# LSTM with residual: weight sums read in place, plain-block stores and plain products moved within the first steps

## Chip, core and metric

The kernel runs on one core of a Trainium2 chip. The metric is the device time of one execution in microseconds (us); lower is better. The profile names the engines PE (TensorE), DVE (VectorE), ACT (ScalarE), POOL (GpSimd) and SP (SyncE, which issues every DMA here); "PEld" is TensorE's weight load.

## What is computed

An LSTM over 512 time steps with batch 32 and width 512, whose output is added to its input:

```python
xW = jnp.einsum('ntd,dg->ntg', x, Wx) + b        # x: (32, 512, 512), Wx: (512, 2048)
def step(carry, xw_t):
    prev_h, prev_c = carry
    a = xw_t + prev_h @ Wh                        # Wh: (512, 2048)
    i, f, o = sigmoid of the first three quarters of a;  g = tanh of the last
    next_c = f * prev_c + i * g
    next_h = o * jnp.tanh(next_c)
    ...
out = x + lstm(x, cond_1024, Wx, Wh, b)
```

All data is float32. The steps depend on each other through `prev_h`; `xW` does not.

## The kernel before

**A step.** `h_part(t)` (L252) makes the hidden-state product: 32 matmul records on line 261 that add to a PSUM bank which already holds step t's row of xW plus bias. That row was copied there by `seed_step` (L692, ACT, line 699) from the small ring `xw`. `cell(t)` (L265) then runs the gates on ACT (L276 to L278, L283) and DVE (L280 to L287) and ends with the transposed state `ht` (L287), for which the next `h_part` waits. While the cell runs, TensorE works at the input product of later steps: that work is the "stream".

**The stream.** Steps 20 to 499 get their xW from 15 groups of 32 steps. A group is made by a fast bilinear scheme with 26 "slots". A slot multiplies one sum of x blocks (U, table `U_SUMS`, made on DVE at L476) by one sum of weight blocks (V, table `V_SUMS`) in seven products; DVE evacuates the results into `cbuf` and `r1` buffers with help of ACT (`evacuate`, L609: ACT L618, L627, L634; DVE L624, L628, L631) and combines them into output blocks (`w_op`, L402; DVE line 423), which go to DRAM (`xwd`, L439) and come back row by row (`load_xw`, L679). `items` (L531) lists all products in order: "row" n of this list holds the first two products of slot n, two of slot n-1, two of slot n-2 and the last of slot n-3, so that a full row has seven. `emit_matmuls(n)` (L541) issues the next n quarters of products (four quarters are one product, 8 records on line 562), and `pos` counts the quarters. `u_ahead(n)` (L603) makes the U sums that the next n quarters need. `seed_banks` (L586) copies bias seeds into the banks of some slots (`BIAS_OF`, ACT line 595).

**The weight sums.** V sums do not depend on the group: they are made once, in the first steps (`v_sum`, L758; DVE lines 734 and 737), in temporary rooms (`vroom`, L703; `V_ROOMS` says which room each sum takes), stored to DRAM (`v_store`, L740, L741), and read back for every group as ring rows (`load_v`, L649; three rows `vring`; lines 662 and 667). Eight slots (`V_DIRECT`) use a plain weight block instead of a sum; their parts come straight from Wx (L662) or are stored by `v_raw` (L765).

**The first 20 steps (the head).** Their xW is a plain product with bias: `plain_block` (L189, line 197). Steps 0 to 4 are done at the start; steps 5 to 19 come as listed in `HEAD_PLAINS`, two whole blocks in each of steps 0 to 4, one in steps 6 to 9. `HEAD_STREAM` (L45) gives the number of quarters streamed in each step from step 5 on; together 728, all of group 0. Each step is cut into chunks (L932 to L944): 24 quarters (16 in step 5), then a plain block, then at most 12 quarters at a time. `jobs` (L877 to L886) hangs the early DVE work and stores on steps: V sums in steps 0 to 4, the stores of six plain weight blocks in step 6, `late_seeds` (bias combinations, L792, DVE lines 786 to 798) in step 8.

**Order.** The program is scheduled by hand: every engine and SP's queue run their instructions in the order of emission. `room["dve"]` is a count of spare DVE time that decides how many `w_op` are emitted in a chunk.

**The end.** From step 468 the stream is over, and plain products for the last 12 steps (`plain_part`, L201) fill TensorE; their weights are loaded by `late_loads` (L222) at the steps `LATE` (L41).

Of the kernel before, what the change touches and what calls it, by code (L numbers as in the profile page):

```python
# [40 lines left out]
LATE = (453, 455, 457, 463, 465, 467, 469)  # L41
# [3 lines left out]
HEAD_STREAM = (0, 0, 0, 0, 0, 16, 40, 48, 56, 56, 60, 60, 60, 60, 60, 56, 52, 44, 32, 28)  # L45
# [14 lines left out]
V_ROOMS = (5, 0, 1, 2, 6, 3, 4, 0, 1, 2, 3, 7, 0, 6, 1, 4, 5, 2)  # L60
# [44 lines left out]
def kernel(  # L105
# [77 lines left out]
    def raw(blk):  # L183

        if late_weights[0]:
            return late_r[:, LATE_AT[blk]] if blk < 6 else r1[:, blk - 6]
        return r1[:, blk]
# [26 lines left out]

    def late_load(c, a, b):
        rows = wx[c].rearrange("p (j s c) -> p j s c", j=NJ, s=2)
        dst, n = (late_r, LATE_AT[a]) if a < 6 else (r1, a - 6)
        return lambda: nc.sync.dma_start(
            out=dst[:, n : n + b - a, c % 2 * 2 : c % 2 * 2 + 2], in_=rows[:, a % 4 : a % 4 + b - a]
        )  # L220
# [3 lines left out]
    late_loads += [late_load(2, 4, 6), late_load(3, 4, 6), late_load(2, 6, 8), late_load(3, 6, 8)]  # L224
# [86 lines left out]
    free_c = [NC, 0, 2, 4, 5, 8, 1, 3]  # L311
    last_x = []
    free_u = [0, 1, 2, 3, 6, 7, 4, 5]
# [87 lines left out]

    def w_op(short=False):  # L402
        first = wqueue[0]
# [29 lines left out]
        store_blocks()  # L433
# [107 lines left out]
    def emit_matmuls(n):  # L541

        while n > 0 and pos[0] < 4 * len(items):
# [17 lines left out]
            for j in range(4):  # L561
# [3 lines left out]
                    vring[:, row % 3, RIGHT[r], cols],  # L565
# [20 lines left out]
    def seed_banks(n):  # L586

        last = (pos[0] + n - 1) // 4
        while seeded[0] < len(items):
            row, slot, r = items[seeded[0]]  # L590
            if r == 1 and slot % R in BIAS_OF:
                late = seeded[0] > last
                if late and (pos[0] < 4 * bank_free(slot) or (slot - 5, 4) in finished or seeded[0] > last + 10):
                    return
# [54 lines left out]
    def load_v(row):  # L649
# [8 lines left out]
        for n, a, b in parts:  # L658
            while a < b:
                s, e = n - a // 2, b  # L660
                if row < 2 * R and a in (0, 2, 4) and s in V_DIRECT:
# [3 lines left out]
                if row < 2 * R:  # L665
                    e = next((k for k in (2, 4) if a < k < b and n - k // 2 in V_DIRECT), b)
                nc.sync.dma_start(out=vring[:, row % 3, a:e], in_=vdram[n, :, a:e])
                a = e

# [36 lines left out]
    vroom.append(xs0[:, 4:6].rearrange("p k s m -> p (k s m)")[:, 0 : 7 * HW].rearrange("p (k c) -> p k c", k=7))  # L706
# [51 lines left out]
    def v_sum(i):  # L758
        d = v_add(V_SUMS[i])
        vt[i] = d  # L760
        for s in range(R):
            if V_OF[s] == i:
                v_stores.append(lambda s=s: v_store(s, split_parts(vroom[d]), vroom[d]))

    def v_raw(s):  # L765
        v_store(s, v_parts(V_OF[s]))
# [8 lines left out]
    seed_rows = [cbuf[:, 6 + i // 2, i % 2 * 2 : i % 2 * 2 + 2].rearrange("p s c -> p (s c)") for i in range(4)]  # L775
    seed_rows += [seeds_own[:, i] for i in range(2)]
    names = ("-b2", "b0-b3", "b3", "b0-b1+b2", "b1", "b1-b0")
# [13 lines left out]

    def late_seeds():  # L792
        q = seed_rows
        split_seeds((1, 2, 3))
        sub(q[0], q[1], q[4])
        sub(q[1], q[1], q[2])
        add(q[3], q[0], q[3])
        sub(q[0], q[0], q[3])
# [27 lines left out]
    with tc.manual_schedule():  # L826
# [40 lines left out]
        for s in V_DIRECT[:2]:  # L867
            v_raw(s)
# [29 lines left out]
        for t in range(T):  # L898
# [18 lines left out]
            if t == 1:  # L917
# [6 lines left out]
            if t == 7:  # L924
                load_seeds(((1, 0), (3, 2), (2, 3)))
# [5 lines left out]
            if t < HEAD_STEPS:  # L931
# [3 lines left out]
                if t > 4:  # L935
                    chunks.append(("stream", {5: 16}.get(t, 24)))
                    left -= chunks[0][1]
                while plain or left:
                    if plain:
                        chunks.append(plain.pop(0))  # L940
                    m = 0 if plain and t <= 5 else min(left, 12)
                    if m:
                        chunks.append(("stream", m))
# [146 lines left out]
```

## Time and profile before

| what | value |
|---|---|
| median of 3 runs | 3096.03 us (3094.58 to 3096.34) |
| the profiled execution | 3094.41 us, span 3092.6 us |
| TensorE matmul busy | 3065.7 us, 99% of the span, 43600 records |
| DVE, ACT, POOL busy | 2350.3, 1473.6, 241.3 us |
| DMA | 756.94 MB, mean 245 GB/s |

How to read it: a row of the timeline gives start, duration (us), engine, line, operation, operands (out<-in), form and count, and in brackets the idle time before it with what ended it. Consecutive alike instructions are merged into one row. Ends of matmuls are modelled and overlap the next start by some tenths, so prices are best taken from start to start. A row of the table by stretches gives the stretch, its length, busy time and records of PE, PEld, DVE, ACT and POOL, the granted TensorE clock, the busy share of the DMA engines, and GB/s.

### The profile page before, as it was taken

What the parts mean: (1) busy time and instruction counts of PE and PEld (TensorE: products, weight loads), DVE (VectorE), ACT (ScalarE), POOL (GpSimd) and SP (SyncE); (2) the same over time, 40 slices, a digit from 0 to 9 for tenths busy, and PEclk for the clock granted to TensorE, in tenths of its full rate; (3) what the DMA queues carried; (4) which work ended last, traced back from release to release, by engine and by line L of the source; (5) the groups of instructions that cost most, each with busy time, mean ns of one, the idle gap of its engine ahead of it and who ended that gap; (6) DMA issues with size and microseconds to landing.
All of it is one profiled execution on the core that took longest, in us unless ns stands there. A gap on an engine that the chain in (4) does not pass through costs nothing.

```text
span 3092.6 us, 108381 instructions
## 1 busy us (share of the span) xinstructions
PE 3065.7 (99%) x43600; PEld 1654.6 (54%) x43600; DVE 2350.3 (76%) x6381; ACT 1473.6 (48%) x5528; POOL 241.3 (8%) x508
## 2 busy tenths in 40 slices
PE   9899999999999999999999999999999999999998
PEld 7654555555555555555555555555555555555665
DVE  8588787787877878778787787878778787787644
ACT  2344544445454444545445444454445545444444
POOL 0000000000000000000000000000000000000110
PEclk9999999999999999999999999999999999999999
DMA  9788878787777777778788787877878778788530
GB/s 360 253 288 265 280 249 272 236 264 239 250 257 249 256 243 248 260 238 270 235 258 262 226 268 241 260 249 242 266 240 265 238 249 260 246 265 259 170 91 22
DMA packets 320439, 756.94 MB, mean 245 GB/s; under 512 B 51008, under 2 KB 102720, under 8 KB 319424
## 3 DMA queue, kind: packets, MB, share of 16 engines
q1 hardware_dynamic: 319936, 750.00, 75.0%
q8 instruction: 344, 5.64, 0.8%
q14 instruction: 159, 1.30, 0.1%
HBM read 568.13 MB, written 184.81 MB: 243 GB/s over the span
## 4 chain that ended last, share of the span: by engine, by line
PE 94%; DVE 3%; DMA 2%; issue 1%; ACT 0%; SPq 0%; DVEq 0%; ACTq 0%
PE gbank L261 53%; PE xbank L562 32%; PE bbank L562 5%; PE xbank L261 2%; PE xbank L206 1%; DMA r<-in_L_cond_Wx_dram 1%; DMA vdram<-vring 1%; DVE vring L737 0%; DVE ubuf L737 0%; DVE prod L280 0%; PE gbank L197 0%; DMA vring<-vdram 0%; DVE s L281 0%; DMA vdram<-ubuf 0%; DVE ht L287 0%
## 5 line engine op out<-in xcount | busy, mean ns | idle before, releaser
L261 PE MATMUL gbank<-wh_sb,ht 128*32 128x512 f32 (+1 forms) x16288 | 1780.3, 575 | 5.3 <-DVE ht L287 3.4
L261 PEld LDWEIGHTS gbank<-wh_sb,ht 128*32 128x32 f32 x16288 | 606.3, 110 | 834.9 <-issue 703.6
L562 PE MATMUL xbank<-vring,ubuf 128*32 128x256 f32 (+1 forms) x13632 | 855.3, 369 | 8.8 <-issue 5.2
L276 ACT ACTIVATE s<-gbank 128x128 f32<-128x128 f32 x976 | 274.0, 281 | 1222.0 <-PE gbank L261 1221.4
L562 PEld LDWEIGHTS xbank<-vring,ubuf 128*32 128x32 f32 x13632 | 530.6, 110 | 300.4 <-issue 141.4
L280 DVE TENSOR_TENSOR prod<-s 128x128 f32<-128x128 f32 x1024 | 293.9, 287 | 489.1 <-ACT s L277 484.5
L295 POOL TENSOR_TENSOR oc<-xnat,ht 128x128 f32<-128x128 f32 x504 | 241.1, 478 | 2813.4 <-DVE ht L287 1349.8
L283 ACT ACTIVATE tanh_c<-s 128x64 f32<-128x64 f32 x1024 | 262.5, 257 | 244.0 <-DVE s L281 241.4
L287 DVE STREAM_TRANSPOSE ht<-hbuf 128x64 f32<-128x64 f32 x1022 | 250.9, 245 | 76.9 <-DVE hbuf L285 2.9
L699 ACT COPY gbank<-xw 128x512 f32<-128x512 f32 x459 | 275.9, 601 | 4.9 <-DMA xw<-xwd 4.8
L281 DVE TENSOR_TENSOR s<-prod 128x64 f32<-128x64 f32 x1024 | 230.3, 225 | 35.2
L285 DVE TENSOR_TENSOR hbuf<-o,tanh_c 128x64 f32<-128x64 f32 x1024 | 211.9, 207 | 31.3 <-ACT tanh_c L283 30.7
L277 ACT ACTIVATE s<-gbank 128x64 f32<-128x64 f32 x976 | 226.0, 232 | 0.0
L562 PE MATMUL xbank<-vring,xs 128*32 128x256 f32 (+1 forms) x3216 | 209.4, 357 | 3.4 <-DMA vring<-in_L_cond_Wx_dram 1.8
L562 PE MATMUL xbank<-vring,r 128*32 128x256 f32 (+1 forms) x3216 | 208.4, 357 | 0.0
L562 PE MATMUL bbank<-vring,ubuf 128*32 128x256 f32 (+1 forms) x2608 | 185.7, 342 | 0.0
L562 PEld LDWEIGHTS xbank<-vring,r 128*32 128x32 f32 x3216 | 123.5, 110 | 78.7 <-issue 46.2
L562 PEld LDWEIGHTS xbank<-vring,xs 128*32 128x32 f32 x3216 | 124.7, 110 | 64.0 <-issue 23.8
L423 DVE TENSOR_TENSOR cbuf<-cbuf 128x1024 f32<-128x1024 f32 x130 | 157.9, 1218 | 0.6
L278 ACT ACTIVATE o<-gbank 128x128 f32<-128x128 f32 (+1 forms) x509 | 155.5, 305 | 0.0
L562 PEld LDWEIGHTS bbank<-vring,ubuf 128*32 128x32 f32 x2608 | 102.2, 110 | 66.5 <-issue 38.3
L423 DVE TENSOR_TENSOR r<-r 128x1024 f32<-128x1024 f32 x104 | 127.5, 1226 | 0.8
(136 smaller groups left out, 2546.9 us busy)
## 6 DMA issues: line engine op xcount, KB each, us to landing
vring<-vdram SPq DMA_DIRECT2D x311, 896.0 KB, 5.7
xw<-xwd SPq DMA_DIRECT2D x1920, 64.0 KB, 4.4
xwd<-r SPq DMA_DIRECT2D x116, 512.0 KB, 4.7
xwd<-cbuf SPq DMA_DIRECT2D x114, 512.0 KB, 4.7
out_dram<-oc SPq DMA_DIRECT2D x255, 128.0 KB, 4.2
xnat<-in_x_dram SPq DMA_DIRECT2D x62, 512.0 KB, 6.6
xs<-in_x_grouped_dram SPq DMA_DIRECT2D x45, 512.0 KB, 4.5
vring<-vdram SPq DMA_DIRECT2D x35, 512.0 KB, 5.0
```

Source lines behind the costliest of these rows:

```text
L261: nc.tensor.matmul(dst[j * B : (j + 1) * B], state["ht"][:, k], m, start=False, stop=True, skip_group_check=True)
L276: nc.scalar.activation(s[:, u, 0:2], g[:, n_, 0:2], AF.Sigmoid)
L277: nc.scalar.activation(s[:, u, 2], g[:, n_, 3], AF.Tanh)
L280: nc.vector.tensor_mul(prod[:, u], s[:, u, 0:2], s[:, u, 2:4])
L281: add(nxt[:, u, 3], prod[:, u, 0], prod[:, u, 1])
L283: nc.scalar.activation(tanh_c[:, HALVES[u]], nxt[:, u, 3], AF.Tanh)
L285: nc.vector.tensor_mul(hbuf[:, HALVES[u]], o[:, u], tanh_c[:, HALVES[u]])
L287: nc.vector.transpose(ht[:, 2 * u : 2 * u + 2].rearrange("p q b -> p (q b)"), hbuf[:, HALVES[u]])
L295: (nc.gpsimd if t < T - 8 else nc.vector).tensor_add(oc[:, tt % 2], x_of(t), ht)
L423: op(c_of(dst), c_of(src), c_of(bb))
L562: nc.tensor.matmul(dst[j * B : (j + 1) * B, cols], left_of(gr, s, r)[:, j * B : (j + 1) * B], vring[:, row % 3, RIGHT[r], cols], start=sta ...
L699: nc.scalar.copy(bank_of(t), src)
```

## The change

1. The first four slots (`HELD = 4`) read their weights where they were made: sums 9 and 10 in their rooms (vring 0, ubuf 6 and 7), plain blocks 5 and 0 in r1 and cbuf. No ring rows are loaded for them in group 0, and buffers that hold them come free with their last product. `V_ROOMS` is new, with two more rooms in `xs0`; the x rows 0 and 1 load in step 2 instead of 1.
2. The stores of all plain blocks, and of sums 9 and 10, which later groups need, move to steps 5 to 7. Before, two plain blocks were stored ahead of step 0, six in step 6, and the two sums when they were made.
3. From step 5 on, a plain product comes in four pieces, each followed by a share of the stream; `HEAD_STREAM` has other numbers with the same sum.
4. Seeds: one in step 8, the rest in step 10, in other buffers. `seed_step` of the next step is emitted ahead of the first stream chunk's matmuls (for step 20, behind cell 19) instead of at the end of the step. In the head, finished output blocks are stored at the start of a chunk instead of at once.
5. The last late weights load into free buffers at step 468 instead of 469 into r1.

The diff, cut to its core:

```diff
-LATE = (453, 455, 457, 463, 465, 467, 469)
+LATE = (453, 455, 457, 463, 465, 467, 468)
-HEAD_STREAM = (0, 0, 0, 0, 0, 16, 40, 48, 56, 56, 60, 60, 60, 60, 60, 56, 52, 44, 32, 28)
+HEAD_STREAM = (0, 0, 0, 0, 0, 24, 52, 48, 56, 56, 56, 56, 56, 56, 56, 56, 48, 44, 36, 28)
+HELD = 4
-V_ROOMS = (5, 0, 1, 2, 6, 3, 4, 0, 1, 2, 3, 7, 0, 6, 1, 4, 5, 2)
+V_ROOMS = (5, 0, 6, 8, 1, 3, 9, 2, 4, 7, 3, 2, 7, 4, 1, 3, 2, 5)
...
+    def last_load(c):
+        rows = wx[c].rearrange("p (j s c) -> p j s c", j=NJ, s=2)
+        while len(late_more) < 2:
+            late_more.append(buf_of(take(free_c)))
+        for n in range(2):
+            nc.sync.dma_start(out=late_more[n][:, c % 2 * 2 : c % 2 * 2 + 2], in_=rows[:, 2 + n])
...
-    free_c = [NC, 0, 2, 4, 5, 8, 1, 3]
+    free_c = [NC, 2, 4, 1, 3, 6, 7]
-    free_u = [0, 1, 2, 3, 6, 7, 4, 5]
+    free_u = [0, 1, 2, 3, 4, 5]
...
     def w_op(short=False):
+        if short and done_blocks:
+            store_blocks()
+            return
...
-        store_blocks()
+        if not wait_to_store[0]:
+            store_blocks()
...
-                    vring[:, row % 3, RIGHT[r], cols],
+                    right_of(row, slot, RIGHT[r])[:, cols],
...
                 if r == 4:
                     left_done(gr, s)
+                    if slot < HELD:
+                        (free_u if slot == 1 else free_c).extend({1: (6, 7), 2: (V_OF[2],), 3: (V_OF[3],)}.get(slot, ()))
+
+    def right_of(row, slot, k):
+        if slot >= HELD:
+            return vring[:, row % 3, k]
+        return v_parts(V_OF[slot])[2] if k == 6 else v_parts(V_OF[slot])[k % 2][:, k // 2]
...
                 s, e = n - a // 2, b
+                if row < 2 * HELD and s < HELD:
+                    a = min(a + 2, b)
+                    continue
...
-            if V_OF[s] == i:
+            if V_OF[s] == i and s >= HELD:
                 v_stores.append(lambda s=s: v_store(s, split_parts(vroom[d]), vroom[d]))
...
-        for s in V_DIRECT[:2]:
-            v_raw(s)
...
-        jobs[3] = [lambda: load_v_to(1)] + [lambda: pair_sum(0, (0, 1))] * 4 + [lambda: u_ahead(8)] + sums(24)
+        jobs[3] = [lambda: pair_sum(0, (0, 1))] * 4 + [lambda: u_ahead(8)] + sums(24)
-        jobs[6] = [lambda s=s: v_raw(s) for s in V_DIRECT[2:]]
-        jobs[8] = [late_seeds]
-        jobs[9] = [lambda: load_row(0, 3), lambda: free_c.extend(range(NC + 1, NC + 7))]
+        raws = lambda *ids: [lambda s=s: v_raw(s) for s in ids]
+        jobs[5] = raws(0, 7, 17, 24)
+        jobs[6] = raws(1, 8, 15, 21)
+        jobs[7] = raws(2, 3)
+        jobs[8] = [second_seeds]
+        jobs[10] = [late_seeds]
...
-            if t == 1:
+            if t == 2:
                 load_row(0, 0)
                 load_row(0, 1)
...
+                pieces = [(k, p, cs) for k, p in plain for cs in (((0, 1, 2, 3),) if t < 5 else ((0,), (1,), (2,), (3,)))]
+                while pieces or left:
+                    m = min(left, 12)
+                    if pieces:
+                        chunks.append(pieces.pop(0))
+                        m = -(-left // (4 * len(pieces) + 4)) * 4
                     if m:
-                        chunks.append(("stream", m))
+                        chunks.append(("stream", m, None))
                         left -= m
...
                         load_v_ahead()
+                        store_blocks()
                         u_ahead(m)
...
                         seed_banks(m)
+                        if i == 0 and t + 1 in SEEDED and t + 1 < HEAD:
+                            seed_step(t + 1)
                         emit_matmuls(m)
                         room["dve"] += m * PROD / 4
                         if i == 0:
                             cell(t)
+                            if t + 1 == HEAD:
+                                seed_step(t + 1)
                             room["dve"] -= 2500.0
                             while todo and not plains:
                                 todo.pop(0)()
...
-                if t + 1 in SEEDED:
-                    seed_step(t + 1)
```

`second_seeds` splits one bias row and makes one seed (3 DVE operations); the new `late_seeds` splits two rows and makes the other three seeds (5 operations).

More of the change, by code (lines that the diff above doesn't have):

```diff
@@ L593, in seed_banks @@
                 if late and (pos[0] < 4 * bank_free(slot) or (slot - 5, 4) in finished or seeded[0] > last + 10):
+                    return
+                if BIAS_OF[slot % R] not in seeds_made:
+                    assert late
                     return
@@ L665, in load_v, with known @@
                 if row < 2 * R:
-                    e = next((k for k in (2, 4) if a < k < b and n - k // 2 in V_DIRECT), b)
+                    e = next((k for k in (2, 4, 6) if a < k < b and known(row, n - k // 2, k)), b)
                 nc.sync.dma_start(out=vring[:, row % 3, a:e], in_=vdram[n, :, a:e])
                 a = e
+    def known(row, s, k):
+        return row < 2 * HELD and s < HELD or k < 6 and s in V_DIRECT
     def load_v_to(row):
@@ L946 @@
                 todo = jobs.pop(t, [])
-                plains = sum(k == "plain" for k, _ in chunks)
-                for i, (kind, m) in enumerate(chunks):
+                plains = sum(k == "plain" for k, *_ in chunks)
+                for i, (kind, m, cs) in enumerate(chunks):
                     if kind == "plain":
-                        room["dve"] = 3000.0
-                        for cc in range(4):
+                        room["dve"] = max(room["dve"], 0.0) + PLAIN * len(cs) / 4
+                        for cc in cs:
                             plain_block(m, cc, plain_bank(m), True)
@@ L960 @@
                             flush_v()
+                        if not plains:
+                            for f in ends.get(t, ()):
+                                f()
                     else:
                         load_v_ahead()
+                        store_blocks()
                         u_ahead(m)
@@ L1000 @@
             n = target
+            wait_to_store[0] = False
             if t == HEAD_STEPS:
```

51 lines of the change are left out of this document (33 added, 18 removed).

## The prediction

> **What bounds the kernel now.** The page comes first, then a table by step (each stretch runs from the start of one step's hidden-state product to the next), then TensorE's timeline.
>
> ```profile
> PE 3065.7 (99%) x43600; PEld 1654.6 (54%) x43600; DVE 2350.3 (76%) x6381; ACT 1473.6 (48%) x5528; POOL 241.3 (8%) x508
> ```
> ```profile
> 29.55:81.25 51.70, 51.70 (x806) 38.41 (x801) 46.50 (x90) 14.82 (x50) 5.07 (x5) 1.00 1.03 370
> 81.25:87.82 6.57, 5.85 (x71) 2.41 (x62) 2.77 (x9) 2.74 (x10) 0.00 (x0) 1.00 0.97 353
> 87.82:102.70 14.88, 11.64 (x176) 6.79 (x180) 4.71 (x16) 4.27 (x14) 0.91 (x2) 1.00 0.85 289
> 102.70:116.76 14.06, 12.35 (x199) 8.89 (x193) 5.55 (x18) 4.62 (x14) 0.46 (x1) 1.00 1.05 350
> 116.76:132.99 16.23, 13.18 (x215) 9.32 (x209) 10.70 (x25) 4.30 (x14) 0.46 (x1) 1.00 0.51 167
> 155.83:166.82 10.99, 10.16 (x159) 6.74 (x152) 9.98 (x24) 5.71 (x17) 1.15 (x1) 1.00 1.03 390
> 206.34:216.82 10.48, 9.46 (x140) 4.31 (x136) 9.24 (x21) 4.23 (x15) 0.46 (x1) 1.00 0.77 262
> 225.03:234.62 9.59, 7.40 (x100) 3.26 (x96) 7.08 (x18) 3.16 (x12) 1.15 (x1) 0.96 0.79 272
> 234.62:243.40 8.78, 8.02 (x93) 3.71 (x85) 4.96 (x15) 3.74 (x13) 0.46 (x1) 0.85 0.82 253
> 260.00:2880.00 2620.00, 2619.32 (x36232) 1372.27 (x36228) 2056.81 (x5581) 1288.44 (x4793) 204.72 (x445) 1.00 0.79 253
> ```
>
> TensorE is full in steps 0 to 4 (first row) and again from 260 us on (last row: 0.7 us idle in 2620). The change takes no matmul away, so it can win only what steps 5 to 19, rows two to nine, lose against full TensorE. The price of a full step comes from rows without a wait:
>
> ```profile
> 139.01 3.71 PE L197 MATMUL gbank<-r,xnat 128*32 128x256 f32 x64
> 142.46 1.55 PE L562 MATMUL xbank<-vring,ubuf 128*32 128x256 f32 x24
> ...
> 145.92 3.69 PE L261 MATMUL gbank<-wh_sb,ht 128*32 128x512 f32 x32
> 149.35 1.98 PE L562 MATMUL xbank<-vring,ubuf 128*32 128x256 f32 x32
> 151.08 0.69 PE L562 MATMUL xbank<-vring,xs 128*32 128x256 f32 x8
> ```
>
> Start to start, a plain block is 3.45 us, the hidden-state product 3.43, and 32 records (16 quarters of HEAD_STREAM) 1.73, so 0.108 a quarter. Step 6 (40 quarters, one plain block) should take 11.20 and took 14.88. In this way the steps lose: 5: 1.41; 6: 3.68; 7: 2.00; 8: 3.30; 11: 1.08; 16: 1.43; 18: 2.70; 19: 2.33; the rest to step 20 0.70 together. Sum **18.63 us**. What ended the larger waits:
>
> ```profile
> 94.15 0.64 PE L562 MATMUL xbank<-vring,xs 128*32 128x256 f32 x8 [1.83 <-DMA vring<-in_L_cond_Wx_dram]
> 110.26 0.64 PE L562 MATMUL xbank<-vring,ubuf 128*32 128x256 f32 x8 [1.71 <-DMA vring<-vdram]
> 129.97 2.37 PE L562 MATMUL xbank<-vring,ubuf 128*32 128x256 f32 x40 [3.05 <-issue]
> 214.56 1.93 PE L562 MATMUL xbank<-vring,ubuf 128*32 128x256 f32 x32 [0.70 <-DVE ubuf L476]
> 233.42 1.50 PE L562 MATMUL xbank<-vring,ubuf 128*32 128x256 f32 x16 [2.19 <-issue]
> 243.40 3.64 PE L261 MATMUL gbank<-wh_sb,ht 128*32 128x512 f32 x32 [0.76 <-ACT gbank L699]
> 2897.66 0.41 PE L206 MATMUL xbank<-r,seeds_own 128*32 128x256 f32 x2 [0.42 <-DMA r<-in_L_cond_Wx_dram]
> ```
>
> Three kinds stand here: rows of weight sums that land late (steps 5 to 7); sums of x blocks that VectorE makes late (L476 in step 16; I read the two marked "issue" likewise, since the sum of row 128.78, below, ends 0.1 before TensorE restarts at 129.97); and a seed copy.
>
> **The change, part by part.**
>
> *Rows of the first four slots go.* Nothing is loaded for slots 0 to 3, and row 4, the first load left, is issued at the end of step 5 and needed only in step 7. The row waits of steps 5 to 7 go. Reading weights from r1 or cbuf costs nothing: the plain block (139.01) streams them at 54 ns a record, as the ring is streamed (149.35).
>
> *Stores.* Steps 5 to 7 now issue 2.4, 2.4 and 1.0 MB of them (0.92 MB for a whole sum, 0.52 for a plain weight block). At 370 GB/s (first row) the 2.4 MB ahead of row 4's load are 6.5 us, and step 6 alone lasts over 12: hidden. Uncovered, each late row would cost its own lateness. Loads now stand ahead of finished blocks' stores in SP's queue, which can only bring rows sooner. The x rows move from step 1 to step 2, behind sum 20's store; pair sums need them in step 3, and the two plain blocks of steps 3 and 4 cover a landing some us late: 0.
>
> *Plain blocks in pieces.* TensorE's work is the same, at no price. But a whole plain block gave VectorE 3.45 us between a slot's emission and its first matmul; a piece gives 0.86. What is late next is worked out from these rows of ACT and VectorE:
>
> ```profile
> 151.28 0.57 ACT L618 COPY r<-xbank 128x512 f32<-128x512 f32 x1
> 151.74 0.38 ACT L627 COPY r<-xbank 128x256 f32<-128x256 f32 x1
> ```
> ```profile
> 122.99 0.42 DVE L628 TENSOR_TENSOR cbuf<-xbank,cbuf 128x256 f32<-128x256 f32 x1 [0.20 <-ACT cbuf L627]
> ...
> 123.99 1.09 DVE L786 TENSOR_TENSOR cbuf<-cbuf 128x256 f32<-128x256 f32 x3
> 125.00 0.69 DVE L795 TENSOR_TENSOR cbuf<-cbuf,seeds_own 128x512 f32<-128x512 f32 x1
> ...
> 128.78 1.09 DVE L476 TENSOR_TENSOR ubuf<-xs,ubuf 128x896 f32<-128x896 f32 x1
> ```
> ```profile
> 212.17 0.25 DVE L287 STREAM_TRANSPOSE ht<-hbuf 128x64 f32<-128x64 f32 x1
> ...
> 213.38 1.08 DVE L476 TENSOR_TENSOR ubuf<-ubuf 128x896 f32<-128x896 f32 x1
> ```
>
> The cell frees ACT at 151.28, 5.4 us into a step that began at 145.92; then L618 takes 0.58 and L627 0.35. The three evacuating sums (122.99 to 123.99) are 0.34 each, an L476 sum 1.1. VectorE ends the cell 6.1 us into a step (206.34 to 212.42).
>
> - Step 5 (16 + 8 quarters): slot 0's third product needs L618, at 5.4 + 0.6 + 0.1 = 6.1; TensorE is there at 3.43 + 1.73 = 5.16. **1.0**.
> - Step 6: slot 3 needs sum 17, made after the first piece's evacuation: 5.4 + 0.9 + 3 x 0.34 + 1.1 + 0.1 = 8.6; TensorE is there at 3.43 + 2.59 + 0.86 = 6.9. **1.8**.
> - Step 7: sum 18 likewise, one product (0.43) later. **1.35**.
> - Steps 8 and 9: sums 8, 14 and 19 are made ahead. **0**.
>
> *Seeds.* Three operations move to step 8, under plain pieces. The other five (2 x 0.36 + 3 x 0.66 = 2.7) now follow cell 10, where no plain block covers them. Then come two evacuations (0.7) and sum 11 (1.1): 6.1 + 2.7 + 0.7 + 1.1 + 0.1 = 10.6. Slot 11 starts at quarter 272, 36 into the step: 3.43 + 3.89 = 7.3. **3.3**, much as step 8 lost before.
>
> *HEAD_STREAM.* With 56 quarters, two rows exactly, slots 13 and 15 (sums 20 and 21) start 12 quarters after the sum's emission, as slot 23 did in step 16 (sum 24 at 213.38, restart 214.56 after a useful end at 213.68: 0.88). **0.9 each in steps 11, 12 and 16**. Step 18 again meets the next group's two sums; before, TensorE stood from 225.03 + 6.02 = 231.05 to 233.42, 2.37; four quarters more lie ahead now: 2.37 - 0.43 = **1.9**.
>
> *Earlier seed copies* remove the 0.76 of row 243.40 and step 16's small one; ACT does them during the hidden-state product. About 0.9 of small losses stay.
>
> *Late weights.* The last load moves a step earlier, past the final blocks' stores in SP's queue; its 0.42 goes. If those stores still held it, nothing would be won.
>
> *Early sums with other rooms.* Sum 20 now follows sum 17 in one room, three sums later, and so adds a wait: on VectorE the step's cell stands behind it, and the next hidden-state product waits for that.
>
> ```profile
> 48.37 1.55 DVE L737 TENSOR_TENSOR vring<-cbuf,vring 128x768 f32<-128x768 f32 x2
> ...
> 54.33 0.96 DVE L737 TENSOR_TENSOR vring<-r,ubuf 128x768 f32<-128x768 f32 x1 [0.40 <-DMA vdram<-vring]
> ...
> 58.15 0.24 DVE L287 STREAM_TRANSPOSE ht<-hbuf 128x64 f32<-128x64 f32 x1
> ```
> ```profile
> 55.78 0.94 SPq L741 DMA_DIRECT2D vdram<-vring  x2
> ```
> ```profile
> vdram<-vring SPq DMA_DIRECT2D x5, 768.0 KB, 8.3
> ```
> ```profile
> 60.57 3.70 PE L261 MATMUL xbank<-wh_sb,ht 128*32 128x512 f32 x32
> ```
>
> Sum 17 is ready at 49.9, but its store was issued at 55.78: SP ran 5.9 us behind. Ahead of it 2.9 MB of stores (sums 9 and 10, plain blocks 5 and 0) are now gone, 7.8 us at 370 GB/s, so SP should issue at once. It then lands between 52.4 (2.5 for the bare 0.9 MB) and 58.2 (the 8.3 of a full queue). Up to 56.4 costs nothing (60.57 - 2.0 for the cell - 2.2 for sum 20); 58.2 costs 1.8. I take **0**, since the queue is no longer full.
>
> *The clock.* In windows of 3.41 us:
>
> ```profile
> 128.11:131.52 3.41, 1.55 (x31) 1.17 (x35) 2.86 (x3) 0.42 (x1) 0.00 (x0) 1.00 0.37 142
> 230.51:233.92 3.41, 1.22 (x28) 0.56 (x24) 3.34 (x8) 1.60 (x4) 1.15 (x1) 1.00 1.02 376
> 233.92:237.34 3.42, 3.42 (x28) 1.33 (x24) 2.66 (x4) 0.58 (x1) 0.00 (x0) 0.50 0.81 282
> ```
>
> With TensorE busy for 1.22 us of a window, the next ran at half clock, 1.7 us lost (in steps 18 and 19); with 1.55 it did not. At two of three positions against the windows, step 10's 3.3 idle puts 2.2 (3.41 - 1.22) into one of them, so I count **1.7** once more; step 18's 1.9 is too short.
>
> **Sum.** New losses: 1.0 + 1.8 + 1.35 + 3.3 + 3 x 0.9 + 1.9 + 0.9 + 1.7 = 14.65. Gain 18.63 - 14.65 + 0.4 = 4.4. The profiled execution took 3094.41 (span 3092.6), so **3090.0 us**. The runs shown have the median 3096.03, 1.6 above it. A measurement of this kernel can tell about 0.2% (6.2 us, to 3089.8) from no change; the forecast lies on that edge.
>
> **Rivals.**
>
> 1. *The clock stays open in step 10*: 3088.3. For it: row 128.11, where 3.05 idle was split between windows. [...] Row 233.92 speaks against: a window with 1.22 us of work was enough.
> 2. *The new waits on sums do not show*: of the terms only 0.9 (step 16), 1.9 and 0.9 stay, 3.7 in all: 3094.4 - 14.9 - 0.4 = 3079.1. Against it: the emission order puts each sum behind the cell, as in rows 213.38 and 129.97.
> 3. *Sum 20 waits a little*: +1.8, 3091.8.
> 4. *Slower: SP stays as late as before.* The store issues at 55.78 and lands at 64.1; sum 20 and the cell end at 68.2 where row 60.57 needed them: 7.6 idle and one closed window, 3099.3. It decides from a landing at 60.8 on (4.4 past 56.4). Against it: the 2.9 MB less.
>
> That the change does not do what it says can only mean that a moved row still ends last; the cover above (6.5 of 12 us) leaves that no room.
>
> **How the numbers follow.** Forecast 0.45, rivals 0.18, 0.12, 0.14, 0.11. Faster by over 0.2%: rivals 1 and 2 and 0.17 of the forecast, on the edge: 0.47. Slower by over 0.2% (3102.2): worse cases of rival 4, with further late stores, 0.08. Within: 0.45. The range 3083.0 to 3094.5 holds the forecast, rivals 1 and 3, and part of 2.
>
> **What would show it.** In the profile after, L562 should wait on L476 in steps 6, 7, 10, 11, 12, 16 and 18, on L618 in step 5, and nowhere on vring<-vdram; step 10 holds the longest wait, behind the seed sums; the product at 60.57 starts there. If step 10 shows no wait, the placement of the seeds was misread; if VectorE waits on vdram<-xs near 54, rival 3 or 4 holds.

## The result and the profile after

The changed kernel takes 3090.34 us (median of 20 runs, 3088.48 to 3093.7), the kernel before 3095.26 us (20 runs): ratio 0.9983, 95% interval 0.9976 to 0.999. That is 4.9 us less by the medians. The two profiled executions differ by 3.0 us: 3094.41 before, 3091.39 after (span 3089.6).

The page of the changed kernel and its waits of TensorE (releaser, us in total, number, longest):

```profile
PE 3064.1 (99%) x43600; PEld 1659.5 (54%) x43600; DVE 2350.0 (76%) x6382; ACT 1473.4 (48%) x5528; POOL 240.4 (8%) x508
```
```profile
PE gbank L270 <- DVE ht L296: 4.4, 5, 1.2
PE bbank L577 <- DVE cbuf L649: 3.8, 1, 3.8
...
PE xbank L577 <- ACT cbuf L659: 2.3, 3, 0.9
PE xbank L577 <- issue: 1.7, 1, 1.7
...
PE gbank L270 <- DVE hbuf L294: 1.5, 1, 1.5
PE xbank L577 <- DVE ubuf L491: 1.3, 1, 1.3
PE xbank L577 <- ACT xnat L643: 0.8, 1, 0.8
```

No wait on a weight row (vring from vdram or Wx) is left; waits on VectorE and ACT stand in their place. Lines have moved: the hidden-state product is L270 now, the stream L577, an x sum L491, evacuations L643 to L659, block sums L437. The table by stretches, each cut at starts of hidden-state products (steps 0 to 4, then 5, 6, 7, 8, 10, 11, 16, 18, 19, 20, and the rest):

```profile
29.42:82.61 53.19, 51.97 (x807) 38.19 (x797) 43.89 (x87) 14.47 (x50) 3.69 (x4) 1.00 0.89 319
82.61:89.66 7.05, 6.25 (x81) 2.52 (x84) 5.57 (x15) 4.01 (x13) 1.49 (x2) 1.00 0.84 262
89.66:103.68 14.02, 12.74 (x204) 7.49 (x200) 6.91 (x20) 3.97 (x14) 0.46 (x1) 1.00 1.03 357
103.68:116.86 13.18, 12.31 (x198) 8.98 (x192) 6.28 (x15) 4.91 (x15) 0.46 (x1) 1.00 1.02 352
116.86:129.79 12.93, 12.93 (x214) 10.24 (x208) 8.49 (x19) 4.06 (x14) 0.46 (x1) 1.00 0.41 127
142.72:159.05 16.33, 12.52 (x151) 6.99 (x144) 10.02 (x25) 5.77 (x18) 0.46 (x1) 0.79 0.93 329
159.05:169.41 10.36, 9.65 (x149) 4.58 (x145) 8.18 (x18) 5.17 (x16) 0.46 (x1) 1.00 0.54 155
208.57:218.06 9.49, 8.79 (x132) 4.19 (x128) 8.41 (x20) 3.70 (x14) 0.46 (x1) 1.00 0.58 198
226.25:235.47 9.22, 7.52 (x108) 3.96 (x104) 6.92 (x18) 3.35 (x12) 1.16 (x1) 1.00 0.88 290
235.47:241.93 6.46, 6.46 (x93) 3.45 (x89) 4.25 (x12) 2.78 (x11) 0.00 (x0) 1.00 0.72 221
241.93:249.48 7.55, 6.02 (x85) 3.01 (x78) 7.27 (x18) 3.53 (x13) 0.46 (x1) 1.00 0.79 227
260.00:2878.00 2618.00, 2617.79 (x36225) 1369.14 (x36220) 2055.03 (x5579) 1288.51 (x4793) 204.64 (x444) 1.00 0.78 253
```

With the prediction's prices (3.43 for a hidden-state product, 3.45 for a plain block, 0.108 for a quarter) the loss of each step against full TensorE is its length less that. A step with no loss is at 0.0; step 14 of the changed kernel loses another 0.36, which only the last line counts. The last two columns are a second profile of each kernel, taken in the experiments:

| step | before | predicted | after | after, second | before, second |
|---|---|---|---|---|---|
| 4 | 0.0 | 0 | 1.50 | 0.88 | 0.0 |
| 5 | 1.40 | 1.0 | 1.03 | 1.03 | 0.97 |
| 6 | 3.69 | 1.8 | 1.53 | 1.53 | 6.18 |
| 7 | 1.99 | 1.35 | 1.12 | 1.11 | 0.0 |
| 8 | 3.30 | 0 | 0.0 | 0.0 | 3.30 |
| 10 | 0.0 | 5.0 | 6.85 | 5.54 | 0.0 |
| 11, 12, 16 | 2.52 | 2.7 | 2.66 | 2.66 | 2.52 |
| 18 | 2.71 | 1.9 | 1.91 | 1.91 | 2.37 |
| 19 | 2.32 | 0 | 0.0 | 0.0 | 2.67 |
| 20 | -0.28 | 0 | 1.10 | 1.10 | -0.29 |
| all up to 20 | 18.0 | 14.65 | 18.1 | 16.2 | 18.1 |

So in the first pair of profiles the first 20 steps gain nothing: step 21 begins at 249.57 before and at 249.48 after. The 3.0 us come later. Steps 21 to 454 are 1.3 us shorter (2559.05 to 2557.74), the steps from 455 to the last 1.5. The losses of before come to 18.0 here and to 18.63 in the prediction: its "rest" of 0.70 is 0.4 at its own prices, and step 20, which it left out, is 0.28 shorter than its price.

**Step 10**, TensorE and VectorE:

```profile
153.25 1.08 PE L577 MATMUL bbank<-vring,ubuf 128*32 128x256 f32 x8 [3.81 <-DVE cbuf L649]
```
```profile
148.52 0.25 DVE L296 STREAM_TRANSPOSE ht<-hbuf 128x64 f32<-128x64 f32 x1
149.87 0.43 DVE L821 TENSOR_TENSOR cbuf<-cbuf 128x256 f32<-128x256 f32 x1 [1.11 <-DMA cbuf<-in_L_cond_b_dram]
150.50 0.43 DVE L821 TENSOR_TENSOR r<-r 128x256 f32<-128x256 f32 x1 [0.21 <-DMA r<-in_L_cond_b_dram]
...
152.18 0.68 DVE L839 TENSOR_TENSOR cbuf<-cbuf,r 128x512 f32<-128x512 f32 x1
152.78 0.42 DVE L649 TENSOR_TENSOR cbuf<-bbank,cbuf 128x256 f32<-128x256 f32 x1
```

VectorE ends the cell at 148.8, stands for the seed rows, works on the seeds until 152.8, and only then empties the bank that TensorE needs. The clock then closes for two windows, as the same profile cut at the clock's own windows shows (the granted clock, the share of its full rate that TensorE is given, is the third figure from the end):

```profile
148.61:152.03 3.42, 0.83 (x16) 0.33 (x8) 2.07 (x5) 0.86 (x2) 0.46 (x1) 1.00 1.08 375
152.03:155.44 3.41, 2.19 (x24) 1.02 (x28) 3.41 (x8) 0.19 (x1) 0.00 (x0) 0.50 0.94 374
155.44:158.86 3.42, 3.42 (x40) 1.58 (x36) 2.27 (x5) 1.56 (x4) 0.00 (x0) 0.50 0.74 252
```

**Steps 4 and 20**, in which nothing was lost before. In step 4 VectorE stands 5.16 us ahead of x sum 9, in step 20 three block sums stand ahead of the cell, and TensorE waits for the state:

```profile
76.81 1.09 DVE L491 TENSOR_TENSOR ubuf<-xs 128x896 f32<-128x896 f32 x1 [5.16 <-DMA vdram<-ubuf]
```
```profile
244.31 1.22 DVE L437 TENSOR_TENSOR r<-r 128x1024 f32<-128x1024 f32 x1
245.45 2.48 DVE L437 TENSOR_TENSOR cbuf<-cbuf 128x1024 f32<-128x1024 f32 x2
247.84 0.28 DVE L289 TENSOR_TENSOR prod<-s 128x128 f32<-128x128 f32 x1
```
```profile
249.48 1.06 PE L270 MATMUL gbank<-wh_sb,ht 128*32 128x512 f32 x8 [1.53 <-DVE hbuf L294]
```

### The profile page after: what moved, and what is told of

Same layout as the page of the kernel before. It is cut to its first block, busy times and chain, and to the rows that moved or that the text cites. A ratio compares the mean times of both kernels' runs of the same rounds, so it can differ in the third digit from the quotient of the medians.

```text
span 3089.6 us, 108356 instructions
## 1 busy us (share of the span) xinstructions
PE 3064.1 (99%) x43600; PEld 1659.5 (54%) x43600; DVE 2350.0 (76%) x6382; ACT 1473.4 (48%) x5528; POOL 240.4 (8%) x508
## 4 chain that ended last, share of the span: by engine, by line
PE 95%; DVE 2%; DMA 1%; ACT 0%; issue 0%; SPq 0%; DVEq 0%; ACTq 0%
PE gbank L270 53%; PE xbank L577 32%; PE bbank L577 5%; PE xbank L270 2%; PE xbank L207 1%; DMA vdram<-ubuf 0%; PE gbank L198 0%; DMA r<-in_L_cond_b_dram 0%; DVE prod L289 0%; DVE s L290 0%; DMA vdram<-xs 0%; DVE ubuf L771 0%; DMA xw<-kept 0%; DVE ht L296 0%; DVE hbuf L294 0%
## 5 line engine op out<-in xcount | busy, mean ns | idle before, releaser
L270 PE MATMUL gbank<-wh_sb,ht 128*32 128x512 f32 (+1 forms) x16288 | 1778.7, 575 | 6.1 <-DVE ht L296 4.4
L270 PEld LDWEIGHTS gbank<-wh_sb,ht 128*32 128x32 f32 x16288 | 607.7, 110 | 831.3 <-issue 702.9
L577 PE MATMUL xbank<-vring,ubuf 128*32 128x256 f32 (+1 forms) x13584 | 853.1, 369 | 5.5 <-ACT cbuf L659 2.3
L577 PEld LDWEIGHTS xbank<-vring,ubuf 128*32 128x32 f32 x13584 | 527.7, 110 | 296.5 <-issue 135.1
L292 ACT ACTIVATE tanh_c<-s 128x64 f32<-128x64 f32 x1024 | 262.4, 256 | 255.0 <-DVE s L290 252.3
L437 DVE TENSOR_TENSOR cbuf<-cbuf 128x1024 f32<-128x1024 f32 x181 | 219.3, 1217 | 1.1
L577 PE MATMUL xbank<-vring,r 128*32 128x256 f32 (+1 forms) x3216 | 208.3, 357 | 0.0
L577 PE MATMUL xbank<-vring,xs 128*32 128x256 f32 (+1 forms) x3120 | 203.9, 358 | 0.0
L577 PE MATMUL bbank<-vring,ubuf 128*32 128x256 f32 (+1 forms) x2600 | 185.3, 343 | 3.8 <-DVE cbuf L649 3.8
L577 PEld LDWEIGHTS xbank<-vring,r 128*32 128x32 f32 x3216 | 123.1, 110 | 78.6 <-issue 45.7
L577 PEld LDWEIGHTS xbank<-vring,xs 128*32 128x32 f32 x3120 | 120.9, 111 | 59.0 <-issue 24.0
L643 ACT COPY cbuf<-xbank 128x512 f32<-128x512 f32 x222 | 129.5, 583 | 29.1 <-PE xbank L577 20.6
L577 PEld LDWEIGHTS bbank<-vring,ubuf 128*32 128x32 f32 x2600 | 101.3, 110 | 73.1 <-issue 41.0
```

The source lines that it names most:

```text
L270: nc.tensor.matmul(dst[j * B : (j + 1) * B], state["ht"][:, k], m, start=False, stop=True, skip_group_check=True)
L292: nc.scalar.activation(tanh_c[:, HALVES[u]], nxt[:, u, 3], AF.Tanh)
L437: op(c_of(dst), c_of(src), c_of(bb))
L577: nc.tensor.matmul(dst[j * B : (j + 1) * B, cols], left_of(gr, s, r)[:, j * B : (j + 1) * B], right_of(row, slot, RIGHT[r])[:, cols], star ...
```

## Experiments

The theory to be tested: the rows of the first four slots were worth what steps 5 to 8 lost, and the change gives that back at three places of VectorE, the seeds in step 10, x sums behind the cell, and a store's room in step 4. A, B and C are the theories of each expectation. Medians stand against the kernel before, run beside them on the same chip (3095.0 to 3095.6).

**seeds_out** (changed kernel, no late seeds)

```diff
-        split_seeds((1, 2))
-        sub(q[3], q[1], q[4])
-        sub(q[3], q[3], q[0])
-        sub(q[1], q[1], q[2])
-                lambda: load_seeds(((1, 0), (2, 3))),
```

> The changed kernel without the two late seed loads and the five operations of late_seeds; the seeds of slots 12, 13, 15, 19, 21 and 22 are left out, so those blocks lack part of their bias. In the changed kernel's profile step 10 loses 6.85 us: VectorE stands 1.3 for the seed loads, works 2.7 on the seeds, and TensorE's 3.8 us wait ends behind the two evacuations after them; two clock windows close. Theory A (the seeds' place on VectorE is the cause, the clock follows from it): step 10 loses at most 1 us, no window closes there, and the time falls by 6 us from 3090.3 to about 3084.5. Rival B (the evacuations and sum 11 behind cell 10 are late without the seeds too): step 10 still loses over 3 us and the time falls by 2.7 at most, to 3087.6.

3086.56 us, ratio 0.9974 (0.9964 to 0.9984). Step 10, by the table by stretches:

```profile
142.99:153.95 10.96, 9.73 (x151) 6.56 (x144) 6.36 (x20) 5.55 (x17) 0.46 (x1) 1.00 1.03 358
```

It takes 10.96 instead of 16.33 us: the loss is 1.48, and the clock is 1.00. So the late seeds, their two loads and five operations ahead of the evacuations on VectorE, are the cause and the clock follows from it (A). The rest, 1.48, was half a us above what A allowed (TensorE waits 1.23 for ACT's seed copy, L620), and the time fell by 3.8, not 6: this step won 5.4 against the first profile of the changed kernel, but 4.1 against its second, in which one window closed instead of two (after_again, below).

**sums_ahead** (changed kernel, x sums of 52 quarters in the first chunk)

```diff
-                        u_ahead(m)
+                        u_ahead(m + 28 if i == 0 else m)
```

> The changed kernel with the x sums of the next 52 instead of 24 quarters emitted in a step's first chunk, ahead of the cell. Theory A (these sums stand behind the cell on VectorE, which is idle during most of the hidden-state product): the losses of steps 6 (1.52), 7 (1.12), 11, 12 and 16 (0.88 each) and 18 (1.90), 7.2 us in all, fall below 2 together; the time falls by about 5 us, to 3085. Rival B (the profile names ACT's copies L659 in steps 11, 12 and 16, and L659 is behind the cell too): these three keep 0.5 to 0.9 each. Rival C (a sum ahead of the cell holds the cell up): the following hidden-state products start later by up to 1.1 us a sum and nothing is won, 3090.

3086.76 us, ratio 0.9975 (0.9966 to 0.9984). Steps 6, 7, 11, 12 and 18 lose 0.00 each: A for these, and against B, since ACT's copies kept their places. In step 11 of the changed kernel L659 ended at 167.0 and the sum at 167.2, just ahead of TensorE's restart at 167.25: the profile named the one, the other counted. In step 16 C holds: two sums and three block sums stand ahead of the cell there, which comes 3 us late, and the step loses 3.98 instead of 0.88. The window in which it happened closed the clock:

```profile
208.61:212.02 3.41, 1.54 (x26) 0.72 (x30) 3.04 (x13) 1.53 (x5) 0.45 (x1) 1.00 0.88 246
212.02:215.43 3.41, 3.41 (x35) 1.52 (x31) 2.43 (x4) 1.45 (x3) 0.00 (x0) 0.50 0.89 268
```

**u_order** and **order2** (changed kernel, other rooms for x sums)

```diff
-    free_u = [0, 1, 2, 3, 4, 5]
+    free_u = [2, 3, 0, 1, 4, 5]      # u_order
+    free_u = [4, 5, 2, 3, 0, 1]      # order2
-V_ROOMS = (..., 7, 4, 1, 3, 2, 5)
+V_ROOMS = (..., 7, 4, 1, 3, 2, 3)    # order2
```

> The changed kernel with the x sums' rooms taken in the order 2, 3, 0, 1, 4, 5. Step 4 loses 1.49 us: sum 9 waited 5.2 us on VectorE for the store of weight sum 23 out of rooms 0 and 1, which was issued at 67.0 us. Theory A: in rooms 2 and 3, whose weight sum 21 was stored earlier, no such wait stands; step 4 loses under 0.3 and the time falls by 1.2 to 1.5 us, to 3089. Rival B (the wait moves to the next sum or to the x rows, which cost 0.87 at 69.0): under 0.5 us is won.

> The changed kernel with the x sums' rooms in the order 4, 5, 2, 3, 0, 1 and weight sum 25 in rooms 0 and 1, so that all weight sums keep their values, unlike u_order. Theory A (the wait of sum 9 for the store of weight sum 23 is the whole loss of step 4): step 4 loses under 0.3 instead of 1.49 and the time is 1 to 1.5 us shorter than that of the changed kernel beside it. Rival B (the wait moves to sums in rooms 0 and 1, behind the store of sum 25): steps 5 and 6 lose as much more.

In u_order, which its expectation did not say, weight sum 24 is made after x sums have overwritten sum 21, so slots 23 and 25 (sum 25 is built on sum 24) work with other weights. The times: 3089.38 us, ratio 0.9982 (0.9973 to 0.9991), and 3089.64, 0.9981 (0.9973 to 0.999), the second 1.0 below the changed kernel beside it. VectorE in order2:

```profile
70.92 0.68 DVE L528 TENSOR_TENSOR xs<-xs 128x512 f32<-128x512 f32 x1
71.63 1.09 DVE L491 TENSOR_TENSOR ubuf<-xs 128x896 f32<-128x896 f32 x1
```

The sum follows at once. Step 4 loses nothing in both, and steps 5 and 6 no more than before: A. The size is less sure: the six profiles with the old rooms and the early stores lose 0.5 to 2.1 in step 4, though their programs are the same up to there, and the 1.0 in the medians is little more than their noise. That the wait is the cause is shown by the profile alone.

**rows_back** (changed kernel, rows of slots 0 to 3 from DRAM)

```diff
-HELD = 4
+HELD = 0
+        v_raw(2)
+        v_raw(3)
         for t in range(KEPT):
-        jobs[3] = [lambda: pair_sum
+        jobs[3] = [lambda: load_v_to(1)] + [lambda: pair_sum
```

(The buffers of these slots join `free_u` and `free_c` at the start, and their four stores leave steps 5 to 7.)

> The changed kernel with the rows of slots 0 to 3 read from DRAM again: weight sums 9 and 10 are stored when made, plain blocks 5 and 0 ahead of step 0, and rows 0 and 1 are loaded in step 3; all else stays as changed. Theory A (the rows of the first four slots were what ended the waits of steps 5 to 7): waits of TensorE on the ring appear again in steps 5 to 7, 3 to 6 us in all, and the time rises by as much, to 3093.5 to 3096.5. Rival B (the order of stores and loads in SP's queue was the cause, and that stays changed): under 1 us comes back, 3091.

3097.58 us, ratio 1.001 (1.0001 to 1.0019): 7 us come back, one more than A allowed. Only 2.2 of it is a wait of TensorE on the ring, in step 6. Step 4 loses 3.10 through VectorE, and the window it leaves nearly empty (82.54 to 85.95, 0.58 us of TensorE work) closes the clock over the next one (0.50 from 85.95 to 89.37), so that step 5 loses 2.52:

```profile
72.35 0.69 DVE L522 TENSOR_TENSOR xs<-xs 128x512 f32<-128x512 f32 x1 [1.64 <-DMA xs<-in_x_grouped_dram]
...
79.95 1.09 DVE L491 TENSOR_TENSOR ubuf<-xs 128x896 f32<-128x896 f32 x1 [4.97 <-DMA vdram<-ubuf]
```

The x rows come at 72.35 instead of 69.03, and everything in SP's queue behind them too. So A is right about what the first four slots are worth, and wrong about the path: the extra transfers delay x rows and stores that VectorE waits for, more than the rows themselves. For the x rows these are the four stores alone, since SP issues the first ring load at 77.61, behind them. The run moves rows and stores together; what each is worth by itself was not tried.

**whole** (changed kernel, plain blocks in one piece)

```diff
-... for cs in (((0, 1, 2, 3),) if t < 5 else ((0,), (1,), (2,), (3,)))]
+... for cs in ((0, 1, 2, 3),)]
```

> The changed kernel with the plain products of steps 6 to 9 as one whole block each instead of four pieces amid the stream. Theory A (the working of the prediction: a whole block gives VectorE 3.45 us between a slot's emission and its first product, a piece 0.86): sums 17 and 18 are ready in time, steps 6 and 7 lose nothing instead of 1.52 and 1.12, and the time falls by 2.6 us from 3090.3, to 3087.7. Rival B (the pieces give the evacuations their time, which 28 quarters in a row behind a whole block do not): waits on evacuations of 2 us and more come in steps 6 to 9, and the time stays or rises, 3090 to 3094.

3091.03 us, ratio 0.9985 (0.9976 to 0.9993). Steps 6 and 7 are full, as A says:

```profile
90.44:102.94 12.50, 12.50 (x205) 8.21 (x201) 6.24 (x19) 3.97 (x14) 0.46 (x1) 1.00 1.02 358
102.94:115.00 12.06, 12.06 (x198) 9.35 (x192) 6.35 (x16) 4.68 (x15) 0.46 (x1) 1.00 1.02 339
```

Yet the time did not fall. In its profile steps 4, 14, 18 and 20 lose 0.4 to 1.1 more than the changed kernel's (together 2.7), and a window closes behind step 20 (the clock is 0.96 over step 20; step 21 takes 7.19 instead of 5.80). Step 4 comes ahead of the edit, so its 0.6 can only be the spread between executions. B's waits in steps 6 to 9 did not come. Why the later steps lose more was not tried. One difference stands in the traces: steps 8 and 9 hold four block sums (L437) instead of eight, and steps 14 and 18 five and three instead of four and one. What is shown is that the pieces cost the 2.6 us in steps 6 and 7, and that the kernel as a whole gets nothing for undoing them.

**tail_alone** (kernel before, last late weights as changed)

```diff
-LATE = (453, 455, 457, 463, 465, 467, 469)
+LATE = (453, 455, 457, 463, 465, 467, 468)
-late_load(2, 6, 8), late_load(3, 6, 8)]
+lambda: last_load(2), lambda: last_load(3)]
```

> The kernel before with the last late weights alone changed: loaded at step 468 into free buffers. Theory A (the prediction: only the 0.42 us wait at 2897.66 goes): 3094.7. Theory B (in the profile of the changed kernel steps 469 to 470 are 0.98 us shorter, and from step 471 to the end another 0.5): the profile shows 10.8 us for these two steps instead of 11.76, and the time is 1.0 to 1.5 us shorter, 3093.5 to 3094.

3092.8 us, ratio 0.9993 (0.9984 to 1.0002): 2.8 less by the medians, an interval that holds no change too. The profile decides: steps 469 and 470 take 10.78 us instead of 11.76 (B), and the steps behind them another 0.3. (The profiled execution as a whole took 3095.45; a wait of 1.9 us for a ring row in step 30 is in it alone.) SP's queue shows why; the last load of before, and of the changed kernel:

```profile
2892.57 1.13 SPq L218 DMA_DIRECT2D r<-in_L_cond_Wx_dram  x1
```
```profile
2886.72 0.90 SPq L229 DMA_DIRECT2D cbuf<-in_L_cond_Wx_dram  x2
```

It leaves 5.9 us earlier by the span and 4.5 earlier against step 469, which the changed kernel reaches 1.4 us sooner. The 0.42 in the row of before was not all that the late load cost: it is the only gap of these two steps in the profile, yet they are 0.98 longer.

**before_again** and **after_again** (both kernels, unchanged)

> The kernel before, unchanged, profiled a second time. In its first profile steps 6 and 8 lost 3.69 and 3.30 us and the clock closed once, in step 19; in the profile of tail_alone, whose first 20 steps are the same program, they lost 5.06 and 4.98 and the clock closed in these two steps instead. Theory A (the closing of the clock depends on where an idle time falls against the windows, so the first steps differ by some us between executions of one program): the losses up to step 20 add up to something between 17 and 20 again, with at least one closed window, not necessarily in the same step. Rival B (the first profile is the rule): 18.0 in all, one window, in step 19.

> The changed kernel, unchanged, profiled and timed again. Its first profile closed two windows in step 10 (loss 6.85); u_order, rows_back, sums_ahead and whole lost 5.80, 6.62, 5.15 and 5.00 there with one or two. Theory A (place against the windows): step 10 loses 5.0 to 6.9, one or two windows closed; the time is 3090 to 3091. Rival B: step 10 always loses 6.85.

before_again took 3094.52; its first 20 steps lose 18.1 again, but in step 6 6.18 (two closed windows) and in step 7 nothing, while tail_alone, the same program there, lost 5.06 and 4.98 in steps 6 and 8. The windows of before_again in step 6:

```profile
90.90:94.31 3.41, 1.52 (x27) 0.42 (x16) 2.00 (x9) 1.62 (x8) 0.46 (x1) 1.00 0.77 234
94.31:97.72 3.41, 2.45 (x24) 1.17 (x25) 0.00 (x0) 0.59 (x1) 0.00 (x0) 0.50 0.88 287
97.72:101.14 3.42, 3.42 (x36) 1.62 (x32) 1.42 (x2) 0.86 (x2) 0.00 (x0) 0.50 1.08 377
```

after_again took 3090.62 (median of 11; ratio 0.9985, 0.9976 to 0.9994); its profiled execution, 3089.56, closed one window in step 10 (0.50 from 152.37 to 155.78), not two, and its first 20 steps lose 16.2. A in both. Where the idle time of step 10 falls against the windows is worth 1.3 us; with step 4 (1.50 and 0.88) the two profiles of the changed kernel lie 1.9 apart. By the second one the gain is 18.0 - 16.2 + 1.3 + 1.5 = 4.6, close to the 4.9 of the medians.

**seeds_spread**, **best** and **best2** (changed kernel, mended)

```diff
+        split_seeds((0, 1))                    # step 8, row b0 loaded in step 7
-        sub(q[3], q[1], q[4])
-        sub(q[3], q[3], q[0])
+        add(q[3], q[1], q[2])                  # step 13; best2: steps 11, 12, 13
+        sub(q[3], q[3], q[4])
+        sub(q[3], q[3], q[0])
...
+    u_ahead(m + 28 if i == 0 and t not in (15, 16) else m)     # best, best2, with order2's rooms
+    while t > HEAD_STEPS and wqueue and ...:   # best, best2: step 20, none ahead of the cell
     cell(t)
+    while t == HEAD_STEPS and wqueue and room["dve"] > 1000:   # best, best2: step 20, behind it
+        w_op()
...
+    if i == (0 if t < 10 else 1):              # best2: seeds behind the first evacuations
++    -1300 if t == 15 else -2500                # best2: fewer block sums at the end of step 15
```

> The changed kernel with the late seeds spread out: row b0 is loaded in step 7 and split in step 8, step 10 keeps two operations (split of b3, b0-b3; about 1.0 us instead of 2.7), and the last seed, with one operation more, moves to step 13. Without any seed operation step 10 lost 1.48 us. Theory A: the remaining 1.0 us on VectorE lies partly in its wait for ACT (0.93), step 10 loses 1.5 to 2.5 with no clock window closed, and the time falls by 4.4 to 5.4 us, to 3085 to 3086. Rival B (the wait for the seed rows, 1.3 us, stays, and with it the long idle time): step 10 loses over 3 and a window closes, 3088.

> The changed kernel with four mends: seeds spread as in seeds_spread; x sums of the next 52 quarters ahead of the cell as in sums_ahead, but not in steps 15 and 16; x-sum rooms in the order 4, 5, 2, 3, 0, 1 with weight sum 25 in rooms 0 and 1; in step 20 the block sums behind the cell instead of ahead of it. Expected from the losses in the profile of the changed kernel: step 4 1.5, 6 1.5, 7 1.1, 10 5.9, 11 and 12 0.9 each, 18 1.9, 20 1.1, together 14.8 us less than 3090.3: 3075.5. Rival (VectorE has no room for all of it ahead of the cells, as in step 16 of sums_ahead, which lost 3.98): half of it is lost again, 3082.

> As best, with three more mends: the last seed's three operations go one each to steps 11, 12 and 13, the seed operations from step 10 on behind the first evacuations after the cell, and fewer block sums at the end of step 15. best lost 1.64 in step 10 (TensorE waited 1.36 for an evacuation behind two seed operations), 2.11 in step 13 (1.90 behind three), 2.49 in step 16 (VectorE came 2 us late to the cell). Theory A: these fall to under 0.8 each, and the time by about 4 us from 3083.2, to 3079. Rival B (VectorE is simply full in steps 13 to 17, so the work shows up elsewhere): under 1.5 us is won, 3082.

seeds_spread: 3090.69 us, ratio 0.9985 (0.9977 to 0.9994). Step 10 does what A says (2.46, no window, the clock is 1.00), but the three operations moved to step 13 cost 2.13 there, where nothing was lost before, so the time is the changed kernel's: the expectation priced the move at nothing, and missed. (By its profile the first 20 steps lose 15.6, which is 0.5 to 2.5 less than in the changed kernel; the median does not show it.)

best: 3083.22 us, ratio 0.996 (0.9948 to 0.9973). Steps 4, 6, 7, 12, 18 and 20 lose nothing, but 10, 13 and 16 lose 1.64, 2.11 and 2.49, and what step 20 gains goes to step 21, which takes 7.44 us instead of 5.80. Of the 14.8 us expected 7.1 are won: the rival, that half is lost again, holds, and the time is 1.2 above even its 3082.

best2: **3080.15 us**, ratio 0.9954 (0.994 to 0.9968), 10.5 below the changed kernel beside it. Step 10 loses nothing (9.47 us), step 13 nothing, step 16 1.22; all up to step 20 lose 4.1, and step 21 takes 7.45. Part of what is left moved to step 11 (2.30), where VectorE came late to the cell behind block sums:

```profile
153.75 1.22 DVE L437 TENSOR_TENSOR cbuf<-cbuf 128x1024 f32<-128x1024 f32 x1
154.88 0.28 DVE L289 TENSOR_TENSOR prod<-s 128x128 f32<-128x128 f32 x1
```
```profile
157.12 0.64 PE L577 MATMUL bbank<-vring,xs 128*32 128x256 f32 x8 [1.82 <-DVE cbuf L649]
```

So A for most of it, though 3.1 us were won and not 4, and B for step 11.

## Why the prediction was right, and where it was not

The time forecast (3090.0) is the time measured (3090.34), but the sum behind it is right only in part, and that the two lie so close is luck. It had 4.0 us for the first 20 steps and 0.4 for the end. Measured were 0 to 1.9 and 1.0 there, and 1.8 at places that it did not name. Of these, 1.3 are short stalls of VectorE and ACT that fall elsewhere in the changed program (last section).

- *Rows of the first four slots, and stores*: right. No ring wait is left, the 2.4 MB of stores in step 6 are hidden (the step's DMA share is 1.03, yet TensorE waits for none of it), and rows_back shows 7 us for the slots, rows and stores together.
- *Pieces*: right in cause and size (1.0, 1.8, 1.35 against 1.03, 1.53, 1.12); whole takes steps 6 and 7 to zero.
- *HEAD_STREAM*: right: 0.9 three times and 1.9 against 0.88, 0.90, 0.88 and 1.91. The bet behind it, that the sum and not ACT's copy ends last, is shown by sums_ahead for steps 11, 12 and 18; step 16 lost more there, so for it the bet stays open.
- *Seeds*: the right place, too small: 3.3 and 1.7, together 5.0, against 6.85 and 5.54. The working began the seeds right behind the cell; their rows landed 1.3 us later. And it took sum 11 for the last to come, at 10.6 into the step; the evacuation ahead of it (L649, ended at 10.5) was needed sooner. One closed window was counted; the second came in one profile of the two.
- *Early sums with other rooms: 0*: this step failed. Sum 20, of which it asked, waited 1.86 for sum 17's store and cost nothing, as worked out: the next hidden-state product starts at 60.44, without a wait. VectorE and SP's queue of the changed kernel:

```profile
55.76 0.96 DVE L771 TENSOR_TENSOR xs<-r,vring 128x768 f32<-128x768 f32 x1 [1.86 <-DMA vdram<-xs]
```
```profile
49.83 3.01 SPq L775 DMA_DIRECT2D vdram<-xs  x2
...
66.96 1.07 SPq L775 DMA_DIRECT2D vdram<-ubuf  x2
```

  The wait of sum 20 is the sign that the prediction gave for rivals 3 and 4, but it was not enough to cost anything. The same question was not asked of the x sums: x sum 9 goes into the room of weight sum 23, whose store, issued at 66.96, held it until 76.81; step 4 lost 1.50 (0.88 in the second profile) where the prediction has 0. order2 shows it.
- *Step 20*: the 1.4 us that it loses against before were not in the sum. With the block sums behind the cell, as in best, step 20 loses nothing and step 21 1.6: VectorE then comes late to the next cell, so this loss was moved and not won back.
- *Small losses*: 0.9 was set aside; 0.4 came, nearly all in step 14.
- *Late weights*: 0.42 against 0.98, the mechanism as forecast.
- *The clock*: the reading of row 233.92 held: in the experiments too, windows of 3.41 us with 0.58 to 1.54 us of TensorE work (rows_back, sums_ahead, the others between them) had one at half clock (0.50) behind them.

Rival 1 (no closing, 3088.3) falls by the clock's rows. Rival 2 (sums do not show) falls by sums_ahead, which is 3.6 us faster because they did. Of rivals 3 and 4 the wait that cost something came at another sum; SP was not late: sum 17's store was issued at 49.8, where before it was at 55.8.

## What to carry to other kernels

When a transfer is taken away, look for what its place and its cover were also good for: here the seeds lost the plain block that hid them, and x sums took a room still being stored. Price a moved step at the place where it lands (three operations of 0.7 cost 2.1 in step 13; with one each in steps 11 to 13, steps 12 and 13 lost nothing), and emit what the stream needs next ahead of the cell as long as the engine is idle there. Follow a mend into the step behind it: step 20's loss was gone and stood in step 21. Compare several profiles of one program before you read a difference of two us (the two of the changed kernel lie 1.9 apart).

## What the runs showed of the hardware

The clock's windows: in before the granted clock is 0.50 from 233.92 to 237.34, in after from 152.03 to 158.86, once and twice 3.41 us. Cut at this length from there, no open window with 1.55 us or more of TensorE work closed the next one in the first 270 us of before and after (the least work was 1.55 in before, row 128.11 of the prediction, and 1.88 in after, from 247.61); the one window with less, 1.22 us in before and 0.83 in after, did. So did the windows with 0.74 and 1.54 us in sums_ahead, 1.07 in u_order, 0.58 and 1.05 in rows_back, 1.52 in before_again, 0.99 and 1.03 in tail_alone. A half-clock window with 2.17 us of work in rows_back, 2.19 in after and 2.45 in before_again kept the next one closed; one with 3.12 in u_order, and those with 3.41 and 3.42 in before, after, sums_ahead and rows_back, had an open one behind them. Step 0 begins at 29.55 us in before, at 29.42 in after and at 29.92 in best2, so up to 0.5 us between these profiles lies ahead of step 0.

The 1.3 us between steps 21 and 454 come from single steps that are longer than the same step of the other kernel: eight of before, by 0.25 to 0.33 us, and five of after, by 0.10 to 0.32. In five of the eight a transpose starts 0.46 us late on VectorE though its input is there, as in before:

```profile
413.66 0.23 DVE L285 TENSOR_TENSOR hbuf<-o,tanh_c 128x64 f32<-128x64 f32 x1
414.34 0.24 DVE L287 STREAM_TRANSPOSE ht<-hbuf 128x64 f32<-128x64 f32 x1 [0.46 <-DVE hbuf L285]
```

Before has it at six transposes (414.3, 520.7, 1699.7, 1806.2, 1859.4 and 2936.1; idle 0.46 each), after at three others (785.7, 2176.4 and 2712.6; 0.46 each), each in one of its five longer steps. In the remaining steps, three of before and two of after, it is ACT: a tanh (L283, now L292) starts 0.50 us after the instruction ahead of it and not 0.22. Number the instructions of one engine in a trace from 0, those of its sequencer (semaphores) included. The six transposes of before are VectorE's 831, 1087, 3903, 4159, 4287 and 6847, the three of after 1727, 5055 and 6335; the tanh are ACT's 2623, 3391 and 6335 of before, 959 and 4671 of after. Every one of these numbers leaves 63 when divided by 128. No other transpose of the two profiles behind 270 us starts more than 0.14 us after the instruction ahead of it on VectorE. Not every transpose at such a place is late (VectorE's 2623 and 5951 in before are not, 0.07 to 0.09). VectorE has 7208 such instructions in before and 7213 in after, and its late transposes stand at other instructions. So in these two profiles the stalls go with the count of instructions, and fall elsewhere in the changed program. What makes them was not shown.
